# A set-up stage in a new order and memory layout: half-block opening, A loaded when its buffers come free, four A^T pairs turned between the last features

## The chip, the cores and the metric

One core of one Trainium2 chip runs the whole program. The metric is the device time of one execution in microseconds (us). The engines named here are TensorE (PE in the profile, with its weight loads as PEld), VectorE (DVE), ScalarE (ACT), GpSimd (POOL) and SyncE (SP). SP, ACT and POOL also issue DMAs, each from a queue of its own, in the order of the program.

## The reference, cut to what matters

Two layers work on 4096 nodes with 512 features each. The first, which is all that the change touches, is graph attention with 8 heads of 64 features over a dense 0/1 adjacency matrix A (4096 x 4096):

```
feats = einsum('nf,hfo->hno', X, W)
s_self, s_neigh = einsum(feats, a_self), einsum(feats, a_neigh)      # per head and node
dense = leaky_relu(s_self[:, :, None] + s_neigh[:, None, :], 0.2) * A
out = relu(einsum(softmax(dense), feats) + b)
x1 = layernorm(x + out)
```

The second layer is an attention inside 32 graphs of 128 nodes on x1, with a residual and a layer norm. All is in float32.

## The kernel before, in words

The kernel never forms the 4096 x 4096 scores. Since the exponential of a leaky ReLU of a sum is the larger of two products of exponentials, it needs only columns of exponentials for each node and head, and rows of them. It has a **set-up**, four **passes** (one for each pair of heads, `main_pass(r)`), and the second layer, which is woven into the last pass and follows it.

**Set-up (line 586 to line 830).** x is cut into 8 blocks (`k`) of 4 tiles (`u`) of 128 nodes. For each block `turn_rows` transposes its four tiles on TensorE (16 transposes, L650) and ScalarE copies them to `xT` (L653). `features(k, u)` then multiplies with `w_sb`, the weights W (L722): 8 matrix multiplies, which the profile shows as 16 instructions, into one of two PSUM buffers `ps_fe`. A buffer is freed by the VectorE add of the bias at L733 into `q`. W carries two more columns per head, the weights times `a_self` and `a_neigh`, which VectorE makes by a multiply (L634) and a sum (L635) for each of four chunks of W and each vector; with them the features' product gives the scores too. Tiles 0 to 2 of block 0 don't wait for these columns: `first_scores` (L746) multiplies them later, 16 columns wide. `exponentials` turns scores into exponentials (DVE L664, ACT L670 to L672), `scaled_features` makes the two forms `g` and `f` (`fst`) of the features (L766, L775, L776) and POOL writes them to memory as `g_d` and `f_d` (L789), two tiles at a time. One block later `rows_of_exponentials` and `columns_of_exponentials` transpose the exponentials (L695, L708), and POOL writes rows to `pu_d` (L703).

Loads: SP issues the four tiles of block 0, the two attention vectors, and the bias. ACT issues the four chunks of W and then, for every later block, the four tiles of x, into 4 buffers `xt_f`, each when the block before has left it. POOL loads three blocks of A (`load_adjacency`, L581: 1024 x 512 elements, converted to 8 bits on the way) after blocks 1, 3 and 5.

**A pass.** A pass takes 4 chunks `c` of 1024 rows, and in each 32 tiles `j` of columns, in passes 0 to 2 in groups of 8 (`wide=8`). For a group PE first multiplies `f_s` with the transposed A tile `at` (accf, L1406, 32 instructions), then `g_s` with `q` (acc, L1426, 128 instructions), then the marks with `e_b` (dens, L1441, 32 instructions), and in pass 0 one more sum (ae, L1350). `q` is made by VectorE from a row of exponentials and `at` (L1386), `mark` from `q` by ScalarE (L1395; one in eight by VectorE, L1391). Eight `q` buffers hold four `j`; a new `q` waits for the acc matmul and the mark that read the old one.

In pass 0 the tiles `at` are made from A: `bring` (L1113) transposes a pair of tiles as 16-bit words on TensorE (8 transposes, L1130), ScalarE casts the two tiles of the pair out of PSUM (L1134), and POOL writes them to `at_d` (L1135), from where passes 1 to 3 load them. The first four pairs (`j` 0 to 7) stand at the head of pass 0, behind the whole of set-up; later pairs are turned between the groups, one group ahead. The tiles of `at` go round 12 buffers, of which the last 6 (`more_at`) lie where set-up's buffers were and open only after set-up; the first tile to use them is `j` = 6.

**What sets the order.** PE runs in the order in which it is written (`manual_schedule`). The other engines' instructions are put in order when the program is built, by a scheduler, except where `keep_in_program_order` pins them. Every engine and every DMA queue then works strictly in that order, so that one waiting instruction holds back what is behind it.

Of the kernel before, what the change touches and what calls it, by code (L numbers as in the profile page):

```python
# [404 lines left out]
def adjacency_streamed_path(  # L405
# [144 lines left out]
    def ring(name, pool, n):  # L550

        if name not in more:
            return pool
        k = turns[name] % (n + more[name][1])
        turns[name] += 1
        return pool if k < n else more[name][0]
# [14 lines left out]

    ats = {}
    a_bs = {}
    pools = {}
# [10 lines left out]

    with tc.tile_pool(name="setup1", bufs=1, side="right") as one, tc.tile_pool(
        name="setup2", bufs=2, side="right"
    ) as two, tc.tile_pool(name="xtp", bufs=4, side="right") as xtp, tc.tile_pool(
        name="setup_rows", bufs=1, side="right"
    ) as late, tc.tile_pool(name="staged", bufs=3, side="right") as staged, tc.tile_pool(  # L590
# [9 lines left out]
        def load_rows(k):  # L600
            xts[k] = []
            for u in range(4):
                xt = xtp.tile([P, F], F32, name="xt_f")
                queue = nc.scalar if k else nc.sync
                queue.dma_start(xt, x[ts(4 * k + u, P), :])
                xts[k].append(xt)

        load_rows(0)
        FW = FH + 2
        w_sb = one.tile([P, FC, H, FW], F32, name="w_sb_f")  # L610
        for c in range(FC):
            nc.scalar.dma_start(
                w_sb[:, c, :, :FH], W[:, ts(c, P), :].rearrange("h p o -> p h o")
            )
        a_b2 = staged.tile([P, PR, 2, 2, FP], F32R, name="fst").bitcast(F32)
        a_b2 = a_b2[:, :2].rearrange("p r u s n -> p (r u s n)").rearrange(
            "p (k h o) -> p k h o", k=2, h=H
        )
        for k, v in enumerate((a_self, a_neigh)):
            nc.sync.dma_start(  # L620
                a_b2[:, k].rearrange("p h o -> p (h o)"), broadcast_rows(v, P, H * FH)
            )
        b_row = one.tile([P, H * FH], F32, name="b_row")
        nc.sync.dma_start(b_row, broadcast_rows(b, P, H * FH))
        b_col = one.tile([P, PR], F32, name="b_col")
# [4 lines left out]
        load_rows(1)  # L630
        for c in range(FC):
            prod = qp.tile([P, C], F32, name="q").rearrange("p (k h o) -> p k h o", k=2, h=H)
            for k in range(2):
                nc.vector.tensor_mul(prod[:, k], w_sb[:, c, :, :FH], a_b2[:, k])  # L634
                nc.vector.tensor_reduce(w_sb[:, c, :, FH + k], prod[:, k], AX.X, OP.add)  # L635
# [3 lines left out]
        xs = one.tile([P, FC, NB], F32, name="xs")  # L639

        def turn_rows(k):
            xT = xTs[k] = two.tile([P, FC, 4, P], F32, name="xT_f")
            pts = {}

            order = [(u, c) for u in range(4) for c in range(FC)]
            for u, c in order if k == 0 else sorted(order, key=lambda x: x[1]):
                if u == 0:
                    last = k == 0 and c == FC - 1
                    pts[c] = misc([P, 4, P]) if last else pss.tile([P, 4, P], F32, name="ps_set")
                nc.tensor.transpose(pts[c][:, u, :], xts[k][u][:, ts(c, P)], ident)  # L650
            for c in range(FC):
                pt = pts[c]
                nc.scalar.activation(  # L653
                    xT[:, c], pt, AF.Identity, accum_out=xs[:, c, k : k + 1]
                )

        def exponentials(k, u, sc):

            j = 4 * k + u
            if u == 0:  # L660
                pu_js[k] = two.tile([P, 4, 2, H], F32, name="pu_j")
            st = small.tile([P, 5, H], F32, name="st")
            for lo, hi, w in ((0, 3, 1), (3, 5, 0)):
                nc.vector.tensor_tensor(  # L664
                    st[:, lo:hi].rearrange("p k (q h) -> p k q h", q=2),
                    sc[:, None, :, :, w].to_broadcast([P, hi - lo, 2, H // 2]),
                    powers[:, lo:hi].rearrange("p k (q h) -> p k q h", q=2),
                    OP.mult,
                )
            nc.scalar.activation(e_all[:, j], st[:, 0:2], AF.Exp)  # L670
            nc.scalar.activation(pu_js[k][:, u], st[:, 3:5], AF.Exp)
            nc.scalar.activation(d_all[:, j, :], st[:, 2], AF.Exp)  # L672
# [19 lines left out]
        def rows_of_exponentials(k):  # L692
# [5 lines left out]
            row = rows[k] = late.tile([2 * H, 4 * P], F32, name="pu_row")  # L698
            nc.scalar.copy(
# [5 lines left out]
        def columns_of_exponentials(k):  # L705
            pc = pss.tile([P, 4, 2 * H], F32, name="ps_set")
# [8 lines left out]
        def features(k, u):  # L715
            pf = psf.tile([P, 2, HB], F32, name="ps_fe")
            pf = pf[:, :, : H * FW // 2].rearrange("p q (h w) -> p q h w", w=FW)
            scored = k > 0 or u == 3
            cols = slice(0, FW if scored else FH)
            for c in range(FC):  # L720
                for q in range(2):
# [6 lines left out]
                    )  # L728
            if u % 2 == 0:
# [11 lines left out]
        def first_scores():  # L741

            ps = pss.tile([P, 4, H, 2], F32, name="ps_set")
            for u in range(3):
# [9 lines left out]
            for u in range(3):  # L754
                exponentials(0, u, ps[:, u].rearrange("p (q h) w -> p q h w", q=2))

        def scaled_features(k, u):
# [18 lines left out]
            nc.vector.scalar_tensor_tensor(  # L776
# [6 lines left out]
            )  # L783
            if i:
# [6 lines left out]
        turn_rows(0)  # L791
        for k in range(NB):
            for u in range(4):
                features(k, u)
                if u == (0 if k else 2) and k + 1 < NB:
# [7 lines left out]
                if u == 2 and k == 0:  # L803
# [5 lines left out]
                if k == NB - 1 and u == 0:  # L809
# [3 lines left out]
                    nc.vector.tensor_copy(xsum_b, xsum[:, :, None].to_broadcast([P, FC, 32]))  # L813
                if k == NB - 1 and u == 1:
# [9 lines left out]
        rows_of_exponentials(NB - 1)  # L824
# [5 lines left out]
        columns_of_exponentials(NB - 1)  # L830
# [285 lines left out]
    def bring(r, c, j):  # L1116

        if r:
            at = ats[r, c, j] = ring("at", atp, 6).tile([P, C], F32R, name="at")
            nc.sync.dma_start(at.bitcast(F32), at_d[c, j])  # L1120
            return
        if j % 2:
            return
        if j % 4 == 0 and (c, j) not in a_bs:
            load_adjacency(c, j)
        pairs = a_bs[c, j - j % 4].rearrange("p t n -> p (t n)").bitcast(BF16)
        pairs = pairs.rearrange("p (t k n) -> p t k n", t=CT, k=2)[:, :, j % 4 // 2, :]
        pt = misc([P, CT, P], BF16)
        for t in range(CT):
            nc.tensor.transpose(pt[:, t, :], pairs[:, t, :], ident_b)  # L1130
        both = pt.rearrange("p t n -> p (t n)").bitcast(FP8).rearrange("p (n k) -> p n k", k=2)
        for k in range(2):
            at = ats[r, c, j + k] = ring("at", atp, 6).tile([P, C], F32R, name="at")
            nc.scalar.copy(at, both[:, :, k])  # L1134
            nc.gpsimd.dma_start(at_d[c, j + k], at.bitcast(F32))  # L1135

# [188 lines left out]
    def main_pass(r, ae=None, wide=4):  # L1325

        for c in range(NCH):
            p_row = []
            for h in range(2):
                p_row.append(rowp.tile([P, C], F32, name=f"p_row{h}"))  # L1330
                nc.sync.dma_start(p_row[h], broadcast_rows(pu_d[2 * r + h, ts(c, C)], P, C))
            u_row = urowp.tile([P, C], F32, name="u_row")
            for h in range(2):
                nc.sync.dma_start(
                    u_row[h * FH : (h + 1) * FH, :],
                    broadcast_rows(pu_d[H + 2 * r + h, ts(c, C)], FH, C),
                )
# [23 lines left out]
            for j0 in range(0, NT, wide):  # L1361
# [3 lines left out]
                for k in range(j0 // 4, (j0 + wide) // 4):  # L1365
                    f_s[k] = fsp.tile([P, 4, 2, FP], F32R, name="f_s")
                    nc.sync.dma_start(
                        f_s[k].rearrange("p u s n -> p (u s n)").bitcast(F32), f_d[r, k]
                    )
                    g_s[k] = gfp.tile([P, 4, 2, FH], F32, name="g_s")  # L1370
                    nc.sync.dma_start(g_s[k].rearrange("p u h o -> p (u h o)"), g_d[r, k])
                if at_step == 0:
                    for j in cycle:
                        bring(0, 0, j)
# [6 lines left out]
                for j in cycle:  # L1381
                    for h in range(2):
                        hh = 2 * r + h
                        q = qs[j, h] = ring("q", qp, 6).tile([P, C], F32, name="q")
                        d_j = d_all[:, j, hh : hh + 1]
                        nc.vector.scalar_tensor_tensor(  # L1386
                            q, p_row[h], d_j, ats[r, c, j].bitcast(F32), op0=OP.max, op1=OP.mult
                        )
                        mark = marks[j, h] = sgp.tile([P, C], FP8, name="mark")
                        if j % 4 == 3 and h == 1:  # L1390
                            nc.vector.tensor_scalar(  # L1391
                                mark, q, d_j, None, op0=OP.is_gt, saturate=False
                            )
                        else:
                            nc.scalar.activation(  # L1395
                                mark,
                                q,
                                AF.Sigmoid,
                                bias=nb_all[:, j, hh : hh + 1],
                                scale=BIG,  # L1400
                                saturate=False,
                            )
                for j in cycle:
                    for w in range(2):
                        for s in range(2):
# [6 lines left out]
                            )  # L1412
                if r == 0 and (c, j0 + wide) == (NCH - 1, NT):
# [137 lines left out]
```

## Time and profile before

| | |
|---|---|
| median of 3 runs | 2067.01 us (2066.73 to 2069.36) |
| the profiled execution's own time | 2068.04 us |
| its span, first to last instruction | 2066.2 us |
| PE busy over the span | 2030.9 us (98%) |
| PE busy in 0 to 157 us (set-up) | 146.0 us |
| PE busy in 157 to 194 us (end of set-up, first group of pass 0) | 33.7 us |
| mean granted TensorE clock in these two stretches, and after them | 0.99, 0.86, 1.00 |
| DVE busy, ACT busy over the span | 1670.1 us, 1540.4 us |

The profile is of one execution. In the chain of waits a line holds the start, the length and the instruction or DMA that the end of the chain was waiting for in that stretch. In the stretches a line holds the length, then for each engine its busy time and number of instructions, the granted TensorE clock (1.00 is full), the mean busy share of the DMA engines and GB/s. In a timeline a line holds the start, the length, the engine (a "q" behind the name is its queue, which issues DMAs), the line, what is written and read, the shape and the number of instructions, and in brackets how long the engine was idle before, and what ended that.

### The profile page before, as it was taken

The page shows a single profiled execution, that of the slowest core. Times are in us where ns is not written, and L with a number is a line of the kernel's source. Part 1 is how long each engine was busy: PE and PEld are TensorE (multiplying, and loading weights), DVE is VectorE, ACT ScalarE, POOL GpSimd, SP SyncE. Part 2 cuts the span into 40 slices and gives each one's busy share as a digit, 9 for nine tenths or more (in the row PEclk, how much of TensorE's full clock was granted, in tenths as well). Part 3 has the DMA queues.
Part 4 walks back from the last instruction along what each step waited for, and adds up shares of the span by engine and source line. Part 5 has one row for each costly group of instructions (what it writes and reads, how often), then busy time and mean ns, then how long its engine had stood idle before and what let it go on. Part 6 is the DMA issues. An engine that isn't in the chain of part 4 may idle for free.

```text
span 2066.2 us, 38253 instructions
## 1 busy us (share of the span) xinstructions
PE 2030.9 (98%) x15086; PEld 1049.8 (51%) x15086; DVE 1670.1 (81%) x2125; ACT 1540.4 (75%) x1869; POOL 222.9 (11%) x361
## 2 busy tenths in 40 slices
PE   8999999999999999999999999999999999999997
PEld 6885555444445444444445444444454445445443
DVE  5667888888799998798999899998975884896654
ACT  3338888888878899788899899998885666567420
POOL 1223222222100000000000000000210210210111
PEclk9999999999999999999999999999999999999999
DMA  6989999999899999798999899989974773684211
GB/s 195 303 270 248 270 294 263 296 260 297 264 341 335 367 347 350 258 312 293 327 308 338 300 354 329 329 287 360 315 247 150 240 262 128 229 275 167 74 49 43
DMA packets 207371, 551.31 MB, mean 267 GB/s; under 512 B 24780, under 2 KB 65740, under 8 KB 207180
## 3 DMA queue, kind: packets, MB, share of 16 engines
q1 hardware_dynamic: 136716, 418.45, 58.1%
q0 software_dynamic: 62272, 121.91, 23.1%
q10 hardware_dynamic: 8192, 8.39, 1.2%
q8 instruction: 121, 1.98, 0.4%
q14 instruction: 70, 0.57, 0.1%
HBM read 491.79 MB, written 107.22 MB: 290 GB/s over the span
## 4 chain that ended last, share of the span: by engine, by line
PE 84%; DMA 7%; issue 4%; DVE 2%; ACT 1%; POOL 1%; POOLq 0%; ACTq 0%; DVEq 0%; SPq 0%
PE acc L1426 36%; PE accf L1406 20%; PE ps_m L1067 5%; PE ps_fe L722 5%; PE ps_m L995 5%; DMA at_d<-at 5%; PE dens L1441 5%; PE ps_m L1022 1%; DVE q L1386 1%; PE ps_m L1081 1%; DMA xt_f<-in_x_dram 1%; ACT mark L1395 1%; PE ps_m L975 1%; PE ps_m L1130 1%; PE ps_m L924 1%
## 5 line engine op out<-in xcount | busy, mean ns | idle before, releaser
L1386 DVE SCALAR_TENSOR_TENSOR q<-p_row,d_all,at 128x1024 f32<-128x1024 f32 x1024 | 1241.9, 1277 | 159.9 <-PE acc L1426 129.3
L1395 ACT ACTIVATE mark<-q,nb_all 128x1024 fp8e4<-128x1024 f32 x896 | 995.5, 1145 | 181.4 <-DVE q L1386 165.8
L1426 PE MATMUL acc<-q,g_s 128*32 128x512 f32 x8192 | 904.2, 593 | 1.4 <-DVE q L1386 0.4
L1426 PEld LDWEIGHTS acc<-q,g_s 128*32 128x32 f32 x8192 | 264.3, 110 | 595.3 <-issue 533.6
L1406 PE MATMUL accf<-at,f_s 128*128 128x512 f32 x2048 | 496.7, 398 | 1.9 <-issue 1.8
L1406 PEld LDWEIGHTS accf<-at,f_s 128*128 128x128 f32 x2048 | 380.5, 189 | 111.4 <-issue 28.1
L1151 ACT ACTIVATE ck<-ck,neg_half_f 128x1024 f32<-128x1024 f32 x128 | 146.0, 1141 | 21.7 <-DMA ck<-in_adj_dram 21.7
L1152 ACT ACTIVATE ck<-ck,neg_quarter 128x1024 f32<-128x1024 f32 x128 | 146.4, 1143 | 1.7
L1441 PE MATMUL dens<-mark,e_b 128*6 128x512 fp8e4 x2048 | 125.9, 379 | 0.9 <-ACT mark L1395 0.9
L722 PE MATMUL ps_fe<-w_sb_f,xT_f 128*128 128x264 f32 (+1 forms) x512 | 121.3, 394 | 4.6 <-ACT xT_f L653 4.6
L1134 ACT CAST at<-ps_m 128x1024 fp32r<-128x1024 fp8e4 x128 | 120.1, 1026 | 5.5 <-ACT mark L1395 3.0
L1067 PE MATMUL ps_m<-wvT,x1T 128*128 128x512 f32 x256 | 114.2, 594 | 0.0
L995 PE MATMUL ps_m<-x1T,M_sb 128*128 128x512 f32 x256 | 112.9, 595 | 0.0
L722 PEld LDWEIGHTS ps_fe<-w_sb_f,xT_f 128*128 128x128 f32 x512 | 100.7, 200 | 19.1 <-ACT xT_f L653 5.0
L1271 POOL DMA_DIRECT2D hs_d<-hst x12 | 10.7, 893 | 834.4 <-DVE hst L1261 816.1
L1391 DVE TENSOR_SCALAR mark<-q,d_all 128x1024 fp8e4<-128x1024 f32 x128 | 95.7, 748 | 4.8
L1441 PEld LDWEIGHTS <-e_b 128*6 128x6 bf16 x2048 | 55.8, 86 | 78.5 <-issue 36.2
L1135 POOL DMA_DIRECT2D at_d<-at x128 | 69.0, 539 | 178.0 <-ACT at L1134 107.4
L995 PEld LDWEIGHTS ps_m<-x1T,M_sb 128*128 128x128 f32 x256 | 48.0, 190 | 59.3 <-issue 58.4
L1067 PEld LDWEIGHTS ps_m<-wvT,x1T 128*128 128x128 f32 x256 | 47.6, 190 | 56.4 <-issue 55.1
L1075 DVE TENSOR_TENSOR v_t<-ps_m,bv_row 128x512 f32<-128x512 f32 x32 | 21.7, 683 | 60.5 <-PE ps_m L1067 60.5
L1002 ACT ACTIVATE zT<-ps_m,zb 128x512 f32<-128x512 f32 x32 | 21.8, 680 | 61.1 <-PE ps_m L995 61.1
(185 smaller groups left out, 1084.2 us busy)
## 6 DMA issues: line engine op xcount, KB each, us to landing
at<-at_d SPq DMA_DIRECT2D x384, 512.0 KB, 6.0
f_s<-f_d SPq DMA_DIRECT2D x128, 512.0 KB, 7.5
at_d<-at POOLq DMA_DIRECT2D x128, 512.0 KB, 14.9
ck<-in_adj_dram SPq DMA_DIRECT2D x128, 512.0 KB, 5.4
g_s<-g_d SPq DMA_DIRECT2D x128, 256.0 KB, 5.7
f_d<-fst POOLq DMA_DIRECT2D x16, 1024.0 KB, 7.2
a_b<-in_adj_dram POOLq DMA_DIRECT2D x32, 512.0 KB, 16.3
p_row<-pu_d SPq DMA_DIRECT2D x32, 512.0 KB, 6.7
```

What stands on the lines that cost most here:

```text
L722: nc.tensor.matmul(pf[:, q, :, cols], tile_j(xTs[k][:, c].rearrange("p u n -> p (u n)"), u), w_sb[:, c, 4 * q : 4 * q + 4, cols], start=(c ...
L995: nc.tensor.matmul(pz, L1["M"][:, f, ts(c, P)], x1T[:, f, :], start=(f == 0), stop=(f == FC - 1),)
L1067: nc.tensor.matmul(pv, x1T[:, f, ts(u, P)], L1["wvT"][:, f, :], start=(f == 0), stop=(f == FC - 1),)
L1134: nc.scalar.copy(at, both[:, :, k])
L1151: tc.keep_in_program_order(nc.scalar.activation(ck, ck, AF.Square, bias=neg_half))
L1152: nc.scalar.activation(ck, ck, AF.Abs, bias=neg_quarter, accum_out=binp[:, k : k + 1])
L1386: nc.vector.scalar_tensor_tensor(q, p_row[h], d_j, ats[r, c, j].bitcast(F32), op0=OP.max, op1=OP.mult)
L1391: nc.vector.tensor_scalar(mark, q, d_j, None, op0=OP.is_gt, saturate=False)
L1395: nc.scalar.activation(mark, q, AF.Sigmoid, bias=nb_all[:, j, hh : hh + 1], scale=BIG, saturate=False,)
L1406: nc.tensor.matmul(accf[:, s, :], f_s[j // 4][:, j % 4, w, :], ats[r, c, j][:, ts(s, HB)], start=(j == 0 and w == 0), stop=(j == NT - 1 an ...
L1426: nc.tensor.matmul(acc[o : o + 32, s, :], g_s[j // 4][:, j % 4, h, o % FH : o % FH + 32], qs[j, h][:, ts(s, HB)], start=(j == 0), stop=(j ...
L1441: nc.tensor.matmul(dens[lo : lo + 6, :], e_b[:, j, 2 * r + h, :], marks[j, h][:, ts(s, HB)], start=(j == 0), stop=(j == NT - 1),)
```

## The change

It touches set-up and the head of pass 0 alone; from the second group of pass 0 on the instructions of PE, ACT, DVE and SP are those of before in the same order, and POOL's differ only in where loads of A stand between the writes of `at_d`.

- **Opening.** Block 0 is turned in two halves of two tiles. SP loads tiles 0 and 1, chunks 2 and 3 of W, the two vectors, tiles 2 and 3, the bias, and then all later blocks; ACT loads chunks 0 and 1 of W only. A dummy activation at the start makes ACT load its table then. PE does 9 and 2 transposes of the identity matrix ahead of the first two tiles (`keep_warm`). The order on PE is: half a block turned, features of tile 0 and half of tile 1, the second half turned, the rest of tiles 1 to 3, block 1 turned, the first scores of all four tiles. The extra columns of W are made for chunks 0 and 1 first, and for 2 and 3 behind the bias adds of tiles 0 and 1, in pinned order.
- **A.** When the second pair of a block of A is turned, the load that takes its buffer is issued at once, pinned (`ahead`).
- **End of set-up.** Pairs 0, 2 and 4 of A^T are turned and cast behind the features of tiles 1, 2 and 3 of the last block, pair 6 is turned behind the sums, and the last rows of exponentials after it; pair 6 is cast in pass 0, and the last columns are turned behind the first accf. The first group's `q` and marks are issued behind set-up's last DVE and ACT instructions.
- **Layout and queues.** The set-up pools are stacked in another order; the last row of exponentials lies in `hst`. SP's first loads for pass 0 (`p_row`, `u_row`, `f_s`, `g_s`) are pinned, and so come behind all loads of x. `ring` counts turns from the start, so that the first tile in `more_at` is still `j` = 6.

```diff
+    def turned_steps(c, j, pt):
+        if j % 4 == 0 and (c, j) not in a_bs:
+            load_adjacency(c, j)
...
+        for t in range(CT):
+            nc.tensor.transpose(pt[:, t, :], pairs[:, t, :], ident_b)
+        ahead = c * NT + j + 10
+        if j % 4 == 2 and ahead < NCH * NT:
+            tc.keep_in_program_order(load_adjacency(ahead // NT, ahead % NT))
+        return pt
+    def cast_steps(c, j, pt):
...
+            at = ats[0, c, j + k] = ring("at", atp, 6).tile([P, C], F32R, name="at")
+            ends_of_setup["ACT"] = nc.scalar.copy(at, both[:, :, k])
+            nc.gpsimd.dma_start(at_d[c, j + k], at.bitcast(F32))
...
-                queue = nc.scalar if k else nc.sync
-                queue.dma_start(xt, x[ts(4 * k + u, P), :])
+                nc.sync.dma_start(xt, x[ts(4 * k + u, P), :])
...
-        load_rows(0)
+        load_rows(0, (0, 1))
...
-            nc.scalar.dma_start(
+            queue = nc.scalar if c < FC // 2 else nc.sync
+            queue.dma_start(
                 w_sb[:, c, :, :FH], W[:, ts(c, P), :].rearrange("h p o -> p h o")
             )
+        nc.scalar.activation(neg_quarter, neg_quarter, AF.Identity)
...
+            nc.sync.dma_start(a_s[k], broadcast_rows(v, P, H * FH))
+        load_rows(0, (2, 3))
         b_row = one.tile([P, H * FH], F32, name="b_row")
         nc.sync.dma_start(b_row, broadcast_rows(b, P, H * FH))
+        load_rows(1)
...
+        for c in range(FC // 2):
+            score_columns(c, False)
...
+            def keep_warm(n):
+                pw = psf.tile([P, 2, HB], F32, name="ps_fe")
+                for i in range(n):
+                    nc.tensor.transpose(pw[:, 0, :P], ident, ident)
...
+                if (k, c) == (0, 0) and u < 2:
+                    keep_warm((9, 2)[u])
...
-            scored = k > 0 or u == 3
+            scored = k > 0
...
+                if (k, u, c) == (0, 1, 1):
+                    turn_rows(0, (2, 3))
...
-            for u in range(3):
+            for u in range(4):
...
-        turn_rows(0)
+        turn_rows(0, (0, 1))
         for k in range(NB):
             for u in range(4):
                 features(k, u)
-                if u == (0 if k else 2) and k + 1 < NB:
+                if k == 0 and u < 2:
+                    score_columns(FC // 2 + u)
+                if u == (0 if k else 3) and k + 1 < NB:
                     turn_rows(k + 1)
...
+                if k == NB - 1 and u:
+                    bank = ps0 if u == 1 else pss
+                    pt = bank.tile([P, CT, P], BF16, name="ps_m" if u == 1 else "ps_set")
+                    cast_steps(0, 2 * u - 2, turned_steps(0, 2 * u - 2, pt))
...
-        rows_of_exponentials(NB - 1)
         pS = pss.tile([P, PR], F32, name="ps_set")
         sums_to_columns(pS, S_part)
...
-        columns_of_exponentials(NB - 1)
+        last_pair = turned_steps(0, 6, misc([P, CT, P], BF16))
+        rows_of_exponentials(NB - 1)
+
+    def columns_of_last():
+
+        columns_of_exponentials(NB - 1, misc([P, 4, 2 * H]))
...
                 if at_step == 0:
-                    for j in cycle:
-                        bring(0, 0, j)
+                    cast_steps(0, 6, last_pair)
...
+                if at_step == 0:
+                    columns_of_last()
```

## The prediction

> **What bounds the kernel now.** First the page's busy shares, which say whether any engine leaves time to win:
>
> ```profile
> PE 2030.9 (98%) x15086; PEld 1049.8 (51%) x15086; DVE 1670.1 (81%) x2125; ACT 1540.4 (75%) x1869; POOL 222.9 (11%) x361
> ```
>
> TensorE (PE) is busy for 98%: 35.3 us of the span of 2066.2 are idle. The front table puts most of that in the first 194 us: PE is busy for 179.7 of them, so 14.3 are idle, and the clock is below 1. The change reaches no further than that. Next the waits of PE in the first 200 us (total, times, longest):
>
> ```profile
> PE ps_set L650 <- DMA xt_f<-in_x_dram: 6.4, 4, 3.9
> PE ps_fe L722 <- ACT xT_f L653: 4.6, 1, 4.6
> PE ps_m L1130 <- ACT at L1134: 2.0, 2, 1.2
> PE ps_set L695 <- ACT pu_j L671: 1.3, 1, 1.3
> ```
>
> PE waits for x, once for the first copies of its transposes, and at the end of set-up for the casts and exponentials. The chain of waits up to 180 us shows what lies behind each:
>
> ```profile
> 3.80 8.09 DMA w_sb_f<-in_L_gnn_W_dram
> 11.89 1.28 ACT L653
> ...
> 13.93 12.03 PE ps_fe L722 x48
> ...
> 27.83 3.06 PE ps_set L746 x24
> 30.88 8.75 PE ps_fe L722 x32
> ...
> 77.89 14.75 DMA xt_f<-in_x_dram
> ...
> 165.40 9.75 PE accf L1406 x32
> ```
>
> x is there at 8 us, but ACT stands in the issue of W until 11.89 and then loads its table (1.28), so features start at 13.93. A tile's features are 16 instructions, 3.57 us at full clock; 32 should take 7.14, and take 8.75 after the first scores. One load of x in block 5 takes 14.75 us and stops PE. The stretches (length; PE, PEld, DVE, ACT, POOL busy; granted clock, DMA share, GB/s) show where the clock is halved:
>
> ```profile
> 30.70:33.90 3.20, 3.20 (x8) 2.52 (x9) 0.60 (x6) 1.56 (x10) 0.00 (x0) 0.51 0.66 232
> ...
> 157.00:160.40 3.40, 2.07 (x24) 1.91 (x23) 3.22 (x15) 1.56 (x5) 0.73 (x2) 0.96 0.00 0
> 160.40:170.20 9.80, 7.82 (x38) 6.44 (x36) 9.46 (x14) 9.59 (x10) 4.93 (x9) 0.50 0.90 329
> ```
>
> PE is busy for only 2.07 of 3.40 us as set-up ends, and then has half the clock for 9.8 us. PE's timeline gives the price, and the mark at which I close my sum, the start of the second accf:
>
> ```profile
> 165.16 9.99 PE L1406 MATMUL accf<-at,f_s 128*128 128x512 f32 x32
> ...
> 193.75 7.55 PE L1406 MATMUL accf<-at,f_s 128*128 128x512 f32 x32
> ```
>
> **The change, part by part.** I count against the profiled execution (2068.04, which is 1.03 above the median). Orders on the engines are those of the built programs.
>
> *Opening.* Marks: the end of the last feature of block 0 that stands ahead of the next block, and f(1,0), the first feature of block 1, which starts at 39.63−3.57 = 36.06 now. After: two tiles of x land at 3.8 and 5.6 as now; ACT's half copies (4 × about 0.4, from the 0.57 pitch of whole ones) no longer stand behind the x loads and the table load (issued at the start, some 1.3 us of ACT hidden ahead of x), so features start at about 6.5 instead of 13.93. This is not won in full, since VectorE (DVE) is next. Its 16 multiplies and sums for the score columns wait for a_self, which lands at 8.97 now (6.37 after issue); behind two more loads on SP, I estimate 9.5. Eight have to precede the bias add of tile 0, which frees the first of two PSUM buffers: 9.5 + 8 × 0.61 + 0.2 + 0.7 = 15.3. So PE finishes tiles 0 and 1, waits, and starts tile 2 at 15.3. Then 7.14 (two tiles) + 1.93 (16 transposes) + 4.08 (first scores of four tiles: 32 records for 24, at 3.06/24) = 28.5 for f(1,0): 7.56 won. I take off 1.6 for a half-clock stretch after the first scores as now (8.75−7.14; 0 to 3.4) and 0.4 for a clock that opens late after the wait (now 5 records took 2.50 at the start; 0 to 1.5). **+5.5**, from +3 to +8. The 11 identity transposes (0.23 each at half clock, 2.5) end ahead of x's landing at 3.8; with no cover they cost 2.5.
>
> *Loads of x.* ACT loses 28 issues, about 11 us over set-up; it isn't the bound, so nothing. SP's x loads are now ahead of p_row, u_row, f_s and g_s (3 MB, issued at 45 to 77 now). The 14.75 us load was issued at 77.89, right behind 1.5 MB of p_row and u_row at 73.47 to 76.5; these move behind the last x load, about 105, and are wanted from 160. The 40 us between cover their landings of 6.6 to 14.3. PE's idle of 1.24 there goes: **+1.2** (0.6 to 1.24).
>
> *Pairs 0 and 2 between features.* Each costs PE 0.53 (16 transposes in 1.07) ahead of the last feature's end, F: **−1.06**. Their casts (0.92 each) go to ACT, idle for 3.12 there. The last feature ends at 156.81 now; after at 156.81−5.5−1.2+1.06 = 151.2.
>
> *End of set-up.* Now the second accf comes 193.75−156.81 = 36.94 behind F. After: pair 4 (0.5), sums (0.8), pair 6 (0.5), row transposes (0.44) bring accf to F+2.3 (now F+8.35), with six of eight j cast. Its j = 6 is then reached at F+7.9, and needs the cast of pair 6. That cast writes the first `more_at` buffer, which lies where set-up's last `fst` was, so as now it waits for the landing L of the last f_d write, and ACT, which is in order, holds the row copy ahead of it and the table load (1.28) and every mark behind it. The f_d issue now:
>
> ```profile
> 160.98 0.75 POOL L789 DMA_DIRECT2D f_d<-fst  x1
> ```
>
> This is F+4.2, with 5.7 to landing: F+9.9. After it is issued at F+3.4 by my count; six writes of at_d and a load of A, moved ahead of it in POOL's queue, share the DMA engines, now 0.90 to 1.01 busy from 160 on. Landings of f_d range from 4.9 to 13.5 us, the longest one behind a load of A. So L is F+9 to F+16.9. I take F+13, between the two. From L: accf ends at L+2.85, acc can start at L+4.4, but not ahead of F+16.1, since pair 10's transposes on PE need a buffer that DVE frees only behind eight q's (1.2 each); the marks that dens needs end at L+21.6. The second accf is at F+34.2 for L up to F+10.8, and later one for one from there: +2.75 at best, +0.5 at F+13, −3.4 at F+16.9. PE's wait before j = 6, some 5 us, may start another half-clock window; but accf is then off the path that ends last (ACT's marks), and only what then follows pays. **+0.5**, between +2.75 and −3.4.
>
> Here a rule speaks against the change. The row is the half clock of 160.4 to 170.2, after 3.40 us with 1.33 idle at one time. The Trainium skill, "TensorE: Matmul & The Clock Gate", Part 1, says that about one idle window of 3.4 us throttles the array to half and that about 3.4 us of sustained activity releases it. By the row, a pause much shorter than the 5 us at j = 6 has been enough here; the page's longer window would be filled by it too. The page also would have no throttling at 30.7, where PE was busy in 3.70 of 3.70 us, though with 16-column products; there the row stands. By the page's window one more half-speed stretch would cost 1.7 us, which would make the sum 4.4.
>
> *The rest.* Columns' transposes (0.35) move behind accf, the first tiles' features narrow to 64 of 66 columns for one tile more (0.1 won): nothing. From the second group on the order is that of before, loads of A apart, which find a saturated DMA anyway (each some 5 us); I put ±0.5 on it.
>
> *Sum:* 5.5 + 1.2 − 1.06 + 0.5 = 6.1. The profiled execution would take 2061.9, the median 2060.9.
>
> **The rivals.** A change of 0.2%, 4.1 us, is about what a measurement of this kernel can tell from none.
>
> *B: DVE opens later.* If a_self lands where a_neigh does now (11.78, for chunks 2 and 3 of W go ahead on its queue), the bias add slips by 2.3, and a second half-clock stretch costs 1.7: 2060.9 + 4.0 = 2064.9. For it: W's later chunks took 9.1 and 9.9 us to land. Against: half of W is on another queue.
>
> *C: the cast of pair 6 eats the gain.* At L = F+17 the end of set-up gives −3.5 instead of +0.5; with a half-clock stretch that acc pays (1.7), 2060.9 + 5.7 = 2066.6. For it: 13.5 us landings exist, behind loads of A. Against: the f_d write of now took 5.7.
>
> *E, the other side: the same one wait goes on.* The single mechanism is that landing of f_d at F+13 or later, at 1 us per us. The whole gain is gone at L = F+19.2, and the kernel is slower by 0.2% from L = F+23.3, 20 us after issue; no f_d write took that, though a load of A took 16.5 and an at_d write 20.6. About 2072.
>
> *D: no half-clock stretch* after the first scores, and L by F+10.8: 2060.9 − 1.6 − 2.2 = 2057.1.
>
> That the change doesn't do what it says is a small rival: the orders of the built program show it, and the opening can't fail to start features before 11.89.
>
> **How the numbers follow.** My forecast has 0.55 (its own range 2058 to 2063.5), D 0.10, B 0.20, C 0.10, E 0.05. Faster by over 0.2% means under 2062.9: most of the forecast (0.52) and D, 0.62. Within: B, C and the forecast's upper edge, 0.31; slower 0.07, for E and what I don't see. The range takes D's and C's times with about half a us around them: 2056.5 to 2067.
>
> **What would show it.** First features near 6.5; tile 2's features near 15.3 with PE waiting for DVE's add (L797 after); f(1,0) near 28.5; no wait for x in block 5; last feature's end near 151.2; first accf 2.3 behind it, with a pause before j = 6 that ends when f_d lands; second accf near 187.6. Wrong would be: features' second buffer freed after 17, x loads that stall at SP, or ACT without a mark until F+20.

## The result and the profile after

The changed kernel takes 2073.8 us (median of 8 runs, 2072.11 to 2076.82) against 2067.31 us for the kernel before on the same chip (8 runs, 2066.43 to 2069.36). The ratio is 1.0032, with a 95% interval of 1.0023 to 1.0042: it is slower by about 6.6 us, where 6.1 us less was forecast.

The page's busy shares after the change, in a span of 2071.3 us (2066.2 before):

```profile
PE 2037.5 (98%) x15105; PEld 1052.1 (51%) x15105; DVE 1672.2 (81%) x2125; ACT 1540.6 (74%) x1878; POOL 224.5 (11%) x361
```

The waits of PE in the first 200 us (total, times, longest):

```profile
PE accf L1473 <- ACT at L610: 5.0, 1, 5.0
PE accf L1473 <- ACT hst L761: 1.6, 1, 1.6
PE ps_fe L698 <- POOL ident_f masks.py:199: 1.5, 1, 1.5
PE ps_set L704 <- DMA xt_f<-in_x_dram: 0.5, 2, 0.3
PE ps_fe L784 <- ACT xT_f L707: 0.3, 1, 0.3
```

The waits for x and for the first copies are nearly gone (6.4 and 4.6 before), and a wait of accf for a cast has come. The timeline of PE there, the lines that answer to those of before:

```profile
154.12 7.33 PE L1473 MATMUL accf<-at,f_s 128*128 128x512 f32 x24 [1.59 <-ACT hst L761]
166.47 3.78 PE L1473 MATMUL accf<-at,f_s 128*128 128x512 f32 x8 [5.03 <-ACT at L610]
...
189.47 7.63 PE L1473 MATMUL accf<-at,f_s 128*128 128x512 f32 x32
```

The first accf starts 11.0 us earlier than before (154.12 against 165.16), the second 4.3 earlier (189.47 against 193.75). So at the mark where the prediction closed its sum the change is still a gain. Set side by side, the starts of accf of later groups (a group is 8 tiles `j`; 4 groups make a chunk, 16 make pass 0; counted from 0) show where it went:

| start of accf of group | before, us | after, us | difference |
|---|---|---|---|
| 1 | 193.75 | 189.47 | -4.3 |
| 8 | 377.38 | 373.25 | -4.1 |
| 9 | 404.41 | 406.32 | +1.9 |
| 12 | 485.26 | 487.07 | +1.8 |
| 13 | 511.45 | 517.31 | +5.9 |
| 16 (pass 1) | 592.31 | 598.19 | +5.9 |

Between group 1 and pass 1 the difference moves by 10.2 us, from -4.3 to +5.9. All of this lies in two groups of pass 0, 8 and 12, where it moves by 6.0 and 4.1 us. Each is the first group of a chunk, in which the sums of the chunk before are taken out. PE's timeline at the end of group 8, after and then before:

```profile
398.29 0.38 PE L1510 MATMUL dens<-mark,e_b 128*6 128x512 fp8e4 x1 [0.65 <-ACT mark L1462]
399.33 0.39 PE L1510 MATMUL dens<-mark,e_b 128*6 128x512 fp8e4 x3 [0.66 <-ACT mark L1462]
400.37 0.59 PE L1510 MATMUL dens<-mark,e_b 128*6 128x512 fp8e4 x1 [0.65 <-ACT mark L1462]
401.40 0.59 PE L1510 MATMUL dens<-mark,e_b 128*6 128x512 fp8e4 x3 [0.45 <-ACT mark L1462]
402.44 0.60 PE L1510 MATMUL dens<-mark,e_b 128*6 128x512 fp8e4 x4 [0.45 <-ACT mark L1462]
402.82 1.92 PE L1410 MATMUL ae<-at,e_p 128*25 128x512 bf16 x16
404.68 1.89 PE L599 MATMUL ps_m<-ident_b,a_b 128*128 128x128 bf16 x16
```

```profile
399.57 2.07 PE L1441 MATMUL dens<-mark,e_b 128*6 128x512 fp8e4 x28
402.30 0.39 PE L1441 MATMUL dens<-mark,e_b 128*6 128x512 fp8e4 x4 [0.66 <-ACT mark L1395]
402.51 1.09 PE L1350 MATMUL ae<-at,e_p 128*25 128x512 bf16 x16
403.53 1.07 PE L1130 MATMUL ps_m<-ident_b,a_b 128*128 128x128 bf16 x16
```

After, dens comes to a point where it takes one mark at a time as ACT delivers it (one per 1.04 us). Here the clock is half as well (0.50 in 402.0 to 406.3): the same ae and transposes take 1.92 and 1.89 us in place of 1.09 and 1.07. ACT's timeline says why the marks are late, after and then the copy of before:

```profile
375.34 3.73 ACT L610 CAST at<-ps_m 128x1024 fp32r<-128x1024 fp8e4 x4
387.78 0.58 ACT L1249 COPY hst<-ae 128x512 f32<-128x512 f32 x1 [8.70 <-DMA hs_d<-hst]
388.26 3.23 ACT L1462 ACTIVATE mark<-q,nb_all 128x1024 fp8e4<-128x1024 f32 x3
391.39 3.74 ACT L610 CAST at<-ps_m 128x1024 fp32r<-128x1024 fp8e4 x4
394.99 12.60 ACT L1462 ACTIVATE mark<-q,nb_all 128x1024 fp8e4<-128x1024 f32 x12
```

```profile
387.62 0.59 ACT L1195 COPY hst<-ae 128x512 f32<-128x512 f32 x1 [4.41 <-DMA hs_d<-hst]
```

Behind a chunk's end ACT copies `ae` into the one `hst` buffer (`sums_to_rows`), and must wait until the chunk before has been written from it to `hs_d`. That write was issued 4.1 us earlier than before (372.16, 376.29), as the pass was ahead by that much, but took 15.6 us to land in place of 11.3, and so landed at 387.75 where before it was 387.60. What is ahead of it in POOL's queue are writes of `at_d` and loads of A, and from 190 to 600 us all DMAs of this queue land in the order of their issue, in every profile of this study. The write of `at_d` just ahead of `hs_d` landed at 385.55, before at 385.02. So `hs_d` is late because what is ahead of it is. The waits of POOL from 190 to 560 us, after and then before:

```profile
POOL at_d L611 <- ACT at L610: 240.9, 58, 16.1
...
POOL a_b L587 <- DMA at_d<-at: 2.4, 2, 1.4
POOL a_b L587 <- issue: 2.0, 2, 1.1
POOL a_b L587 <- PE acc L1495: 0.8, 1, 0.8
```

```profile
POOL a_b L581 <- PE ps_m L1130: 100.3, 23, 11.5
POOL at_d L1135 <- ACT at L1134: 72.1, 67, 11.1
```

Before, a load of A was the instruction that POOL waited with, and it went out as soon as PE had turned the last pair of its buffer. After, POOL never waits with a load for PE's transposes (all its waits with a load come to 5.2 us): it waits with a write of `at_d` for one of ACT's casts, and the load stands behind it. The timelines of POOL some 22 us ahead of that `hs_d` show it, after and then before:

```profile
349.30 0.53 POOL L611 DMA_DIRECT2D at_d<-at  x1 [15.53 <-ACT at L610]
350.22 0.53 POOL L611 DMA_DIRECT2D at_d<-at  x1 [0.39 <-ACT at L610]
350.74 1.30 POOL L587 DMA_DIRECT2D a_b<-in_adj_dram  x1
352.03 1.07 POOL L611 DMA_DIRECT2D at_d<-at  x2
```

```profile
350.94 0.90 POOL L581 DMA_DIRECT2D a_b<-in_adj_dram  x1 [9.64 <-PE ps_m L1130]
353.43 0.54 POOL L1135 DMA_DIRECT2D at_d<-at  x1 [1.60 <-ACT at L1134]
354.35 0.53 POOL L1135 DMA_DIRECT2D at_d<-at  x1 [0.38 <-ACT at L1134]
```

So this load went out at the same moment in both, although the pass was 4.1 us further on in the changed kernel. "Issued at once, pinned" is at once in the order of the program, and that order is: cast and write the first pair of a block, turn the second pair, load, cast and write the second pair. The scheduler of the kernel before had put the load ahead of all four writes.

### The profile page after: what moved, and what is told of

Read it like the earlier page. It is cut to its first block, busy times and chain, and to the rows that moved or that the text cites. A ratio compares the mean times of both kernels' runs of the same rounds, so it can differ in the third digit from the quotient of the medians.

```text
span 2071.3 us, 38317 instructions
## 1 busy us (share of the span) xinstructions
PE 2037.5 (98%) x15105; PEld 1052.1 (51%) x15105; DVE 1672.2 (81%) x2125; ACT 1540.6 (74%) x1878; POOL 224.5 (11%) x361
## 4 chain that ended last, share of the span: by engine, by line
PE 77%; DMA 9%; issue 8%; DVE 2%; ACT 2%; POOL 1%; SPq 0%; POOLq 0%; DVEq 0%; ACTq 0%
PE acc L1495 33%; PE accf L1473 18%; DMA a_b<-in_adj_dram 7%; PE ps_m L1142 5%; PE ps_m L1070 5%; PE ps_fe L784 5%; PE dens L1510 4%; PE ps_m L1097 1%; DVE q L1453 1%; PE ps_m L1156 1%; DMA at_d<-at 1%; ACT mark L1462 1%; POOL at_d L611 1%; PE ps_m L1050 1%; DMA hs_d<-hst 1%
## 5 line engine op out<-in xcount | busy, mean ns | idle before, releaser
L610 ACT CAST at<-ps_m 128x1024 fp32r<-128x1024 fp8e4 x124 | 116.2, 1022 | 17.4 <-DVE q L1453 11.3
```

What stands on the lines that cost most here:

```text
L610: ends_of_setup["ACT"] = nc.scalar.copy(at, both[:, :, k])
```

## The experiments

All times are set against runs of the kernel before on the same chip; the ratios carry 95% intervals, and a us figure beside a ratio is the ratio's distance from 1 times 2067. F is the end of set-up's last feature, L the landing of the last write of `f_d`. The last two columns are from one profiled execution of each kernel. F alone differs by up to 3.5 us between kernels with the same code up to the last block's features (150.34 in the changed kernel, 153.87 in no_ahead), so where set-up's end is compared, distances from F are given.

| kernel | ratio to before (95%) | us to before | second accf to before | group 13 to before |
|---|---|---|---|---|
| changed kernel | 1.0032 (1.0023 to 1.0042) | +6.6 | -4.3 | +5.9 |
| no_ahead | 0.9968 (0.9957 to 0.9979) | -6.6 | -4.4 | -4.1 |
| before_ahead | 1.0050 (1.0035 to 1.0065) | +10.3 | 0.0 | +13.2 |
| after_ck | 0.9975 (0.9966 to 0.9983) | -5.2 | -2.9 | -4.6 |
| no_ahead_ck | 0.9952 (0.9939 to 0.9965) | -9.9 | -7.7 | -9.7 |
| load_first | 0.9994 (0.9985 to 1.0002) | -1.2 | -0.2 | +0.1 |
| ahead_setup | 0.9981 (0.9972 to 0.9990) | -3.9 | -2.3 | -1.7 |
| opening_only | 0.9987 (0.9978 to 0.9996) | -2.7 | -2.1 | -1.7 |
| before_ck | 0.9982 (0.9974 to 0.9991) | -3.7 | +0.7 | -1.4 |
| before_load_first | 1.0003 (0.9994 to 1.0012) | +0.6 | -1.3 | +0.4 |
| after_pair6 | 1.0027 (1.0014 to 1.0039) | +5.6 | -5.4 | +3.3 |
| best | 0.9957 (0.9944 to 0.9971) | -8.9 | -9.0 | -11.0 |

**no_ahead: the changed kernel without the pinned loads.**

```diff
-        ahead = c * NT + j + 10
-        if j % 4 == 2 and ahead < NCH * NT:
-            tc.keep_in_program_order(load_adjacency(ahead // NT, ahead % NT))
```

> The changed kernel without its pinned early loads of A (each load of A is issued by `bring` again, in the place that the scheduler gives it). In the changed kernel the second accf starts 4.3 us earlier than before, but group 9 of pass 0 starts 1.9 us later and group 13 5.9 us later. Theory 1, the loads' place in POOL's queue: a pinned load stands behind two writes of at_d that wait for ScalarE's casts, so whenever ScalarE is held up the load is late, the DMA engines run dry for some us, and pass 0 loses what set-up had won and more. Then without the pin group 13 starts at 507 to 510 and the time is 2062 to 2064. Theory 2, the pace of the DMA engines: they are full from 200 to 540 us in the kernel before as well (share 1.04 to 1.14), so A arrives no sooner however early pass 0 begins; then group 13 starts at 511 to 513, and the time is 2066 to 2068, as before.

Measured 2058.85 us, ratio 0.9968. The two steps are gone: the difference to before is -4.4 at the second accf, -4.4 at group 9 and -4.1 at group 13. Three lines are worth 13 us. POOL waits with the load for PE again, and the load that went out at 350.74 in the changed kernel goes out 4.1 us sooner:

```profile
346.62 0.90 POOL L587 DMA_DIRECT2D a_b<-in_adj_dram  x1 [9.24 <-PE ps_m L599]
```

It lands 4.6 us sooner (359.98, 364.57), the write of `at_d` just ahead of `hs_d` 4.8 us sooner (380.77, 385.55), and `hs_d` itself at 383.20, 11.2 us after its issue and 4.4 us earlier than before. So A does come sooner when the pass begins sooner, and theory 2 falls: the DMA engines, however full, do not fix the moment. The time is below theory 1's 2062 to 2064, in part because the kernel before stood at 2065.92 on this chip, and because another us was won late in the last pass, where layer 2 is woven in (-5.1 at its last accf).

**before_ahead: the kernel before, with the pinned loads alone.** The same three lines in `bring`, behind the transposes.

> The kernel before with the pinned early loads of A alone (the set-up is as before). Theory 1: the same holes in the DMA as in the changed kernel, group 13 starts 4 to 6 us later than before, 2070 to 2074. Theory 2: the place of the loads doesn't matter, 2066 to 2068.5.

Measured 2076.8 us, ratio 1.0050. Set-up is untouched (second accf at 193.74). The difference to before moves by 5.9 in group 8 and by 7.1 in group 12. Group 13 so starts 13.2 us later than before, where 4 to 6 were expected, and the time is above the 2070 to 2074 of theory 1. `hs_d` lands 4.3 us later than before (391.87). ACT's and PE's waits there have the same form as in the changed kernel (windows of 300 to 530 and 380 to 530 us):

```profile
ACT hst L1198 <- DMA hs_d<-hst: 17.8, 2, 9.2
```

```profile
PE dens L1444 <- ACT mark L1398: 6.3, 10, 0.7
```

**after_ck: the changed kernel, with `ae` copied elsewhere.** The `ck` buffers are idle in pass 0.

```diff
-            aes = hp_.tile([P, CT, FP], F32, name="hst")
-            aes = aes.rearrange("p t n -> p (t n)")[:, :HB]
+            aes = ckp.tile([P, C], F32, name="ck")[:, :HB]
...
-                spare = hp_.tile([P, CT, FP], F32, name="hst")
+                spare = ckp.tile([P, C], F32, name="ck").rearrange("p (t n) -> p t n", t=CT)
```

> The changed kernel with the copy of `ae` and its scratch in the `ck` buffers (idle in pass 0) in place of the one `hst` buffer, so that ScalarE's copy at a chunk's end no longer waits for the landing of the write of `hs_d`. Theory 1: this wait (8.7 us on ScalarE at 387.8) is what holds up casts, marks and, behind the casts, the pinned loads; without it groups 9 and 13 keep the 4.3 us, 2063 to 2065. Theory 2: the lateness of A turns up at another place, as waits of PE for the casts of late tiles, 2069 to 2073.

Measured 2061.66 us, ratio 0.9975. The loads of A stay where the change put them, `hs_d` still lands 14.9 us after its issue, but nobody waits for it, and the steps turn into gains of 1.2 and 0.4. The time is below the 2063 to 2065 expected, in part for these gains. So the late loads reach PE through this one wait of ACT alone; the tiles themselves are in time.

**no_ahead_ck: both edits.**

> Both edits: no pinned loads of A, and the copy of `ae` in the `ck` buffers. Theory 1: 2061 to 2063, as little left to lose as in set-up's own forecast. Theory 2: 2065 to 2068, since the DMA engines set the pace of pass 0.

Measured 2056.41 us, ratio 0.9952: the fastest of the study by its median ratio, below the 2061 that was expected.

**load_first: pinned, but ahead of the writes.** The writes of a block's first pair are issued behind the load, those of its second pair as well.

```diff
-            nc.gpsimd.dma_start(at_d[c, j + k], at.bitcast(F32))
+            writes.append((at_d[c, j + k], at.bitcast(F32)))
+        while j % 4 and writes:
+            nc.gpsimd.dma_start(*writes.pop(0))
```

> The changed kernel with its loads of A pinned as they are, but ahead of all four writes of at_d of the two pairs (the first pair's writes are issued behind the load). Theory 1 (the place in POOL's queue costs, since ScalarE's casts are ahead of it): the loads are then issued when TensorE frees the buffer, and the time is that of the kernel without pins, 6 to 7 below before: 2059 to 2061. Rival: the two loads that come already in set-up, ahead of the last writes of f_d, cost the time, or the pin as such; then the time stays above that of before, 2070 to 2074.

Measured 2066.22 us, ratio 0.9994. In pass 0 the expectation held: the difference to before is +0.3 at group 2 and +0.1 at group 13, no step at all. POOL waits with the load for PE again:

```profile
POOL a_b L588 <- PE ps_m L600: 107.5, 23, 12.4
```

The time was missed, for a reason in set-up: the edit also moves the two early loads, and accf waits for the cast of pair 6 for 8.2 us (5.0 in the changed kernel), L being F+16.5. The second accf comes at F+40.3, against F+39.1 in the changed kernel and F+35.5 in no_ahead, whose time the expectation took.

**ahead_setup: the pin on set-up's two loads alone** (`c == 0 and j < 8`).

> The changed kernel with the pin on the two loads of A that are issued in set-up only (for the pairs from 12 and from 16); all later loads are issued as before. Theory 1 puts the loss in the many later loads of pass 0: 2058 to 2061, with the wait of accf at j = 6 still near 5 us, as these two loads stand ahead of the last f_d. Rival (the early loads in set-up cost the time): 2070 to 2074.

Measured 2063.14 us, ratio 0.9981. No step of the changed kernel's kind (-2.3 at the second accf, -1.7 at group 13), so the loss of 10 us is in the later loads. It is not as fast as without any pin, nor as the 2058 to 2061 expected: L is F+14.8 and the second accf F+39.0, against F+9.4 and F+35.5 in no_ahead. The two early loads, which stand ahead of the last `f_d`, cost 3.5 us by these profiles and 2.7 by the ratios.

**opening_only: the new opening with the old end of set-up.** From no_ahead: the blocks that turn pairs between the last features, `last_pair`, `columns_of_last` and `issue_after` are taken out, the rows, columns and `bring` stand where they stood before.

> Set-up's opening, loads of x and layout as in the changed kernel, but its end as before: no pins on A, no pairs turned between the last features, the last rows, columns and all four pairs at the head of pass 0. The opening and the stall of x were forecast at 5.5 + 1.2; the first feature of block 1 came 6.1 earlier in the changed kernel. If pass 0 hands this on, as it did without pins, the time is 5.5 to 7 below before: 2060 to 2061.5. If the pace of the DMA engines swallows a part, 2063 to 2066.

Measured 2064.05 us, ratio 0.9987: inside the second branch by its number, but not for its reason. F came at 152.44, 4.4 before the kernel before, but the second accf only 2.1 before it. The scheduler had put three loads behind twelve writes of `at_d` (at 177.12; before, one went out at 171.27 behind eight), and PE waited for one:

```profile
PE ps_m L599 <- DMA a_b<-in_adj_dram: 2.6, 1, 2.6
```

So the opening by itself was not isolated to better than this; it shows once more that the place of these loads is worth some us.

**before_ck: the copy of `ae` elsewhere, in the kernel before.** The edit of after_ck.

> The kernel before with the copy of `ae` and its scratch in the idle `ck` buffers. In the kernel before ScalarE's copy waits three times for the write of `hs_d` (4.4 us at 387.6), but TensorE only 0.9 us in all for marks. If only that reaches TensorE, 2065 to 2067. If casts and loads behind it are late as well, 2061 to 2064.5 (the two kernels without pins differ by 2.4).

Measured 2063.66 us, ratio 0.9982, within the second branch (casts and marks behind the copy). The groups of pass 0 move by 2.4 (from +0.7 to -1.8 at group 14), though only 0.9 us of PE's waits bore the name of a mark.

**before_load_first: the kernel before, pinned and ahead of the writes.** The edits of before_ahead and load_first.

> The kernel before with the pinned loads of A, each ahead of all four writes of at_d of its two pairs. With the pin between the writes the kernel before became 10 us slower, with steps of 6.0 at group 9 and 7.2 at group 13 of pass 0. Theory 1 (place, not pin): no step over 1 us there, 2065 to 2069. Rival (pinned loads as such, or their number in flight): the steps stay, 2074 to 2077.

Measured 2066.67 us, ratio 1.0003: no change that can be told from none, where the same pin between the writes cost 10.3 us. The start of group 9 steps by 1.3 (-1.3 to +0.1) and group 13 by 0.4, somewhat over the 1 us expected at the first. `hs_d` lands at 387.69 (387.60 before). The place is what costs, not the pin.

**after_pair6: the changed kernel, with pair 6's tiles in the `ck` buffers.**

```diff
+            pool = ring("at", atp, 6)
+            if (c, j) == (0, 6):
+                at = ckp.tile([P, C], F32R, name="ck")
+            else:
+                at = pool.tile([P, C], F32R, name="at")
-            at = ats[0, c, j + k] = ring("at", atp, 6).tile([P, C], F32R, name="at")
```

> The changed kernel with the two tiles of pair 6 in the idle `ck` buffers, so that their cast no longer waits for the landing of the last f_d. By the prediction's own sum the second accf then comes 34 to 36 behind the last feature's end (39.1 in the changed kernel, 36.9 before). The steps at groups 9 and 13 should stay, for the loads of A still stand between the writes. If the landing of `hs_d` comes with the pass, the kernel is 3 to 5 faster than the changed one: 2068 to 2071. If it comes when the DMA engines get to it, whatever the pass does, nothing is left of this: 2072 to 2074.

Measured 2071.22 us, ratio 1.0027. The second accf comes at F+35.9, inside the 34 to 36 expected and 3.2 better than in the changed kernel, with L still at F+15.1. The steps stay (+5.4 and +3.2). By the profiles pass 1 starts 2.5 us before the changed kernel's; the ratios (1.0027, 1.0032) are too close to tell the two apart, and the time lies between the ranges of the two branches, so what reaches the end of the 3.2 us stays open.

**best: no_ahead_ck, with tile 3 scored at once.**

```diff
-            if u == 0:
+            if k not in pu_js:
...
-            scored = k > 0
+            scored = k > 0 or u == 3
...
-            for u in range(4):
+            for u in range(3):
```

> No pinned loads of A, the copy of `ae` in the `ck` buffers, and tile 3 of block 0 multiplied with the score columns at once, as before the change (these columns are ready at 22.0, its last chunk comes at 23.4), so that the first scores are 24 records again in place of 32. 8 x 0.128 = 1.0 less, and less of a stretch of narrow products, behind which the clock was halved in most kernels with the new opening (f(1,0) to f(2,0) took 17.3 to 20.2): 1 to 3 below the kernel with the first two edits alone, 2053 to 2056.

Measured 2056.22 us, ratio 0.9957, against 0.9952 without this edit: of the 1 to 3 us expected, nothing that can be measured. Both beat the kernel before and the changed one; no_ahead_ck, the simpler of the two, is the one to keep.

## Why the prediction was wrong, step by step

**Opening (+5.5): right, by luck in two places.** That ScalarE issued W until 11.89 was read wrongly: its issue of W ended at 5.43, and four tiles of x of block 1 held it from 7.39 to 11.86. The change takes the latter away from it, and first features came at 6.75 (6.5 forecast). Tile 2 came at 17.19, not 15.3: the first 10 feature instructions took 4.4 us (6.75 to 11.14, twice the 2.2 of full clock, where 0.4 had been taken off for a late clock), so PE was busy with tile 1 up to 16.9. VectorE's add was through at 16.11; what came last was ScalarE's copy of the second half, 0.26 us behind PE. On the other side the half-clock stretch behind the first scores, for which 1.6 was taken off, did not come in this profile: f(1,0) came at 29.96 (30.5 with both deductions). The first feature of block 2 came at 47.23 against 53.09 before, 5.9 won. In the nine profiles with the new opening it came between 47.23 and 50.76, on average at 49.1, against 53.0 to 54.1 in four with the old one: 4.3 on average.

**Loads of x (+1.2): right.** The stall in block 5 is gone; with the old end of set-up, the way from the first feature of block 2 to F took 102.25 us against 103.71, so 1.5. **Pairs between features (-1.06): right.** With them it took 103.11, 0.9 more.

**End of set-up (+0.5, between +2.75 and -3.4): inside the bounds, mis-sized.** It measured -2.2. The term was L. The last `f_d` was issued at F+3.71 (3.4 forecast) and landed at F+14.9, where 13 was taken. The second accf came at F+39.1 (36.96 before); the prediction's rule (F+34.2, and 1 us per us from L = F+10.8) gives 38.3. The rule itself was tested over a spread: F+34.2 and F+35.5 with L at F+9.4, F+39.0 at 14.8, F+40.3 at 16.5, and F+35.9 where the cast doesn't wait. Rival C's mechanism is real, and what made L late are the two early loads (F+14.8 with them alone, F+9.4 without). The first accf came at F+3.8 and not F+2.3, for the wait of 1.59 on the last row's copy was left out.

**The rest (plus or minus 0.5): this step failed, and cost 10.2 us.** The prediction said that from the second group on the order is that of before, "loads of A apart, which find a saturated DMA anyway (each some 5 us)". The loads did not just meet other DMAs. They were put behind two writes that wait for ACT, so they went out late: at 350.74 in the changed kernel, at 346.62 without the pins, with a pass that was ahead by 4 us in both. `hs_d`, behind them, landed late; ACT, in order, held marks and casts behind its copy; the casts held the next load (394.11, before 386.18). The runs give the price: 10.3 us on the kernel before, 13.2 us between the changed kernel and no_ahead, of which the two early loads in set-up are some 3. No rival covered it: rival E was the right kind of thing, a wait of in-order ACT for a landing, at the wrong place. It was also sized on too few landings: a load of A took 16.5 in the row used, but 20.6 and 23.7 a little later in the same trace (issued at 202.5 and 254.1). The rows that would have shown the failed step were in the trace of before: a load that waits for PE at 350.94 with its four writes behind it, released by ACT, and a wait of 4.4 us of ACT for `hs_d` that had no slack left.

Without the three lines the number would have been met, 6.1 less forecast and 6.6 less measured, but partly by luck. In the profile of no_ahead set-up's last feature came only 2.9 us earlier than before (5.6 forecast), its end gave 1.4 (0.5 forecast), and the last pass gave an us that was not in the sum.

## What to carry to other kernels

Where an edit pins a DMA in program order, look up what then stands ahead of it in its queue and what that waits for; a load that was released by one engine may now be released by another. Price it at the most loaded place of the whole program, not only where the edit is aimed. Look too for waits of an in-order engine that already end last by a hair, such as a single buffer that is refilled when a DMA out of it lands: whatever delays that queue was paid there in full and more (in before_ahead `hs_d` landed 4.3 us later, and group 9 began 6.0 us later). Where a buffer is idle in that phase, using it takes the wait away (3.7 us here, even in the kernel before).

## What the runs showed of the hardware that was not expected

The stretch of half clock behind the first scores comes and goes with the same code. From the first feature of block 1 to that of block 2 took 17.3 us in the changed kernel and in best, and 18.7 to 20.1 in the seven other profiles with the new opening, whose code up to there is the changed kernel's. Two kernels of identical code up to there, the changed one and then no_ahead, in the stretch from 30.60 to 33.80 (length; PE, PEld, DVE, ACT, POOL busy; granted clock, DMA share, GB/s):

```profile
30.60:33.80 3.20, 3.20 (x17) 2.78 (x16) 3.20 (x9) 1.23 (x11) 0.77 (x1) 1.00 0.01 3
```

```profile
30.60:33.80 3.20, 3.20 (x8) 2.51 (x9) 2.99 (x12) 1.46 (x12) 0.10 (x1) 0.50 0.04 12
```

PE was busy without a break in both, with 16-column products from 26.2 to 30.1 in the first and from 26.4 to 30.8 in the second. The Trainium skill, "TensorE: Matmul & The Clock Gate", Part 1, says that the window in which the hardware counts activity runs freely, so that the same kernel differs from run to run in when the clock opens. These two rows show such a difference in when it closes. That narrow products bring it about is only argued: best, with 24 of them in place of 32, had no such stretch, but neither had the changed kernel with 32.

Half a clock also came behind pauses of PE shorter than the 1.33 us ahead of the stretch at 160.4 in the kernel before: five of 0.45 to 0.66 us between 397 and 402.5 us in the changed kernel, with 0.50 in 402.0 to 406.3. But five of 0.56 to 0.66 us between 510 and 515.3 us left the clock at 1.00. So such pauses alone don't decide it, and what does is not shown. Both stretches, in the changed kernel:

```profile
402.00:406.30 4.30, 3.86 (x36) 2.21 (x36) 4.30 (x4) 4.30 (x5) 0.00 (x0) 0.50 1.20 158
510.00:517.00 7.00, 3.82 (x50) 1.50 (x41) 7.00 (x8) 7.00 (x7) 0.00 (x0) 1.00 1.14 234
```
